# Layer 1's experts as seven block products over pairs of token tiles, with combined weights kept split in DRAM

## The chip, the cores and the metric

One Trainium2 chip, one of its cores. The core has five engines that run side by side and each take their own instructions in order: PE (TensorE, matmuls, with weight loads shown apart as PEld), DVE (VectorE), ACT (ScalarE), POOL (GpSimd) and SP (SyncE, which here issues all DMA transfers). The metric is the device time of one execution in microseconds (us), the median over runs.

## The reference

Input `x` is 4 sequences of 512 tokens with 1024 features, in fp32: 2048 tokens, 16 tiles of 128. Two layers follow one another, each with an attention part and an expert part, each behind a layer norm and added to `x`. What the change concerns is the last part:

```
x_q     = x[:, 179:-1, :]                      # x here is the normalised input of this part
routing = softmax(x_q.mean(axis=1) @ router_W.T + router_b)     # one row of 8 weights a sequence
base    = x @ W.T + b                                           # 1024 x 1024
t       = einsum("bsd,erd->bser", x, A)                         # 8 experts, rank 16: 128 columns
lora    = einsum("bser,eor,be->bso", t, B, routing) * 2
out     = base + lora                                           # added to the residual
```

Layer 0's expert part has the same base and low-rank products, but chooses two experts for each token (`route`). Layer 1's attention has 32 heads; its output projection is already computed in seven block products over two token tiles.

## The kernel before

Every product that matters is done in three matmuls (`matmul3`, L128 to L132): each fp32 operand is split into a high part in fp32r and a low rest, and low x high, high x low and high x high are accumulated. A split is a copy on ACT (the high part) and a subtraction on DVE or POOL (the rest).

The stages, in order: layer 0's attention; layer 0's experts, tile by tile (a loop over `order`); shared projections of layer 1's attention; its heads, with weight preparation and the output projection (`project`) interleaved as generators that `advance` steps; layer 1's experts. The scheduler under the kernel places instructions on each engine in nearly this order.

Layer 0's experts, around L430 to L460: per tile, `base` makes three column groups of `po` in PSUM (L130 to L132, 72 matmuls), the first group of tile s+1 before the routing of tile s. `turn0` normalises (`h`, L121) and transposes two tiles ahead (L143, then L125 on ACT and L126 on DVE). POOL adds the bias (L441). `finish` (L330) adds 9 low-rank matmuls to `po` and adds `po` to `x`. Six PSUM banks hold the groups of two tiles, so the first group of tile s+2 needs the bank that L330 of tile s reads. The results go to DRAM as `x_d` (L454). A buffer `raw` of 3072 columns serves as staging room at several places, one use after another; here it holds the weights `waT` from tile 8 on.

Layer 1's experts: its weight `w1` has 1024 + 128 columns and 8 chunks of 128 rows. `fetch_w1` (L668) loads two chunks at a time into `raw` and `prepare_w1` (L673 on ACT, L674 on DVE or POOL) splits them, among the last output projections (`project`, L798 to L847: loads `xs` at L815, split operands `cxh`, `cxl`, additions L843, stores L847). Tiles are loaded (`xt`, L1006), normalised and transposed three tiles ahead (`turn1`). The loop over `s` then runs `base` on three groups of 384 columns, the weighting of the low-rank input (`weigh`), and `finish`, which stores to the output. `mixture` makes the routing of a sequence from the sums of its tiles.

Some numbers of lines in the groups below: L251ff and L221 are layer 0's attention, L743 to L786 the heads of layer 1 (scores, transposes L767, context L783), L882 to L886 the preparation of output weights, L712 and L716 small tables through DRAM.

Of the kernel before, what the change touches and what calls it, by code (L numbers as in the profile page):

```python
# [38 lines left out]
W1_COLS = ((0, 384), (384, 768), (768, 1152))  # L39
# [3 lines left out]
def block_kernel(ctx: ExitStack, tc: tile.TileContext, a: dict, out: bass.AP):  # L43
# [308 lines left out]

    attn = ExitStack()
# [17 lines left out]
    with tc.tile_pool(name="b_h", bufs=2) as hp, tc.tile_pool(name="b_hTh", bufs=2) as hTh, \  # L371
# [54 lines left out]
        po = {0: base(hts[0], w0, W0_COLS, pop, slice(0, 3))}  # L426
        for s, t in enumerate(order):
            if s + 1 < NT:
                po[s + 1] = base(hts[s + 1], w0, W0_COLS, pop, slice(0, 1))
            q, k = divmod(s, NB)  # L430
            hw = weigh(po[s], routed(po[s]), ptp, wk) if s + 1 < NT else hw_last
            if s + 1 < NT:
                po[s + 1] += base(hts[s + 1], w0, W0_COLS, pop, slice(1, 2))
            if k == 1 and q + 1 < TPB:
                with tc.issue_after(normed[1].ins):
                    stats0[q + 1] = statistics([x[:, n * TPB + q + 1, :] for n in range(NB)])
            if s + 2 < NT:
                hts[s + 2] = turn0(s + 2)
            if s == NT - 1:
                hts1[1] = turn1(1, ptp)  # L440
            G.tensor_tensor(x[:, t, :], x[:, t, :], bias0, ALU.add)  # L441
            if s == NT - 2:
                hw_last = weigh(po[s + 1], routed(po[s + 1]), ptp, wk)
            if s + 1 < NT:
                po[s + 1] += base(hts[s + 1], w0, W0_COLS, pop, LAST)
            if s == NT - 2:
# [10 lines left out]
            if s == NT // 2:  # L457
# [203 lines left out]

    W1N = W1_COLS[-1][1]
    w1 = []

    def fetch_w1(ch, room, k):

        r = room[:, k * W1N : (k + 1) * W1N]
        nc.sync.dma_start(out=r, in_=a["w1"][ch])  # L668
        return r

    def prepare_w1(r, pool, eng):
        h, l = (pool.tile([P, W1N], FR, name=f"w1{len(w1)}{q}") for q in "hl")
        A.copy(h, r)  # L673
        eng.tensor_tensor(l, r, f32(h), ALU.subtract)  # L674
        w1.append((h, l))

    with ExitStack() as c2:
# [259 lines left out]
        for u in range(NU + 3):  # L937
# [38 lines left out]
            if u < NU:  # L976
# [8 lines left out]
                if (g, b, i) == (NG - 1, NB - 1, 0):  # L985
                    room = raw()
                    w1_raw = [fetch_w1(k, room, k) for k in range(2)]
# [8 lines left out]
        w1q = dp.enter_context(tc.tile_pool(name="d_wB", bufs=1))  # L996
        hTh = dp.enter_context(tc.tile_pool(name="d_hTh", bufs=4))
        hTl = dp.enter_context(tc.tile_pool(name="d_hTl", bufs=4))
        hp = dp.enter_context(tc.tile_pool(name="d_h", bufs=1))
        xtp = [dp.enter_context(tc.tile_pool(name="d_xA", bufs=4))]  # L1000
        ptp = dp.enter_context(tc.tile_pool(name="d_pt", bufs=2, space=PSUM))

        def fetch(s):
            xs[s] = xt = xtp[s % 6 // 4].tile([P, D], F32, name="xt")
            for k in range(2):
                nc.sync.dma_start(out=xt[:, k * 512 : (k + 1) * 512], in_=x_d[s][k])  # L1006

        xs, hts, sums, rw, po = {}, {}, {}, {}, {}

        def turn1(s):  # L1010
            b, j = divmod(s, TPB)
            h = hp.tile([P, D], F32, name="h")
            normalise(h, xs[s], *stats[s][0], stats[s][1])
            r0, r1 = max(Q_START - j * P, 0), min(Q_END - j * P, P)
            if r0 < r1:
                sums[j] = small.tile([P, ND, 1], F32, name=f"sum{j}")
            hts[s] = transposed(h, (hTh, hTl), ptp, (sums[j], r0, r1) if r0 < r1 else None)

        for s in range(TPB):
            fetch(s)  # L1020
# [4 lines left out]
        stats = {s: (mv, s) for s in range(TPB)}  # L1025
        prepare_w1(w1_raw[0], w1q, V)
        w1_raw += [fetch_w1(2, room, 0)]
        turn1(0)
        prepare_w1(w1_raw[1], w1q, G)
        w1_raw += [fetch_w1(3, room, 1)]  # L1030
        advance(filler, 7)
        turn1(1)
        prepare_w1(w1_raw[2], w1q, V)
        w1_raw += [fetch_w1(4, room, 0)]
# [160 lines left out]
```

## Time and profile before

| | us |
|---|---|
| median of 3 runs | 1829.35 |
| lowest and highest | 1826.6, 1829.43 |
| the profiled execution | 1828.0 |
| its span, first to last instruction | 1826.2 |
| PE busy in the span | 1751.3 (96%) |
| DVE, ACT, POOL busy | 1286.7, 832.1, 803.0 |
| mean granted TensorE clock | 0.991 of full speed |
| DMA moved | 191.33 MB, 105 GB/s in the mean |

The profile is of one execution. Busy times are those of each engine; a busy PE counts matmuls that overlap in its pipeline, so that the pace of matmuls is read from start to start. A row of a group reads: line, engine, operation, output and inputs with their shapes, count, then busy us and mean ns of one, then idle time of that engine just before, with what ended it. A row of the timeline begins with the start and the length in us. SPq stands for the queue of DMA issues. A line number in a group can be that of a helper, such as `matmul3`.

### The profile page before, as it was taken

To read this page: it belongs to the slowest core of one execution; us is meant where nothing else is said; L and a number is where in the kernel's file an instruction comes from. 1 tells how busy PE (TensorE), PEld (TensorE's weight loads), DVE (VectorE), ACT (ScalarE), POOL (GpSimd) and SP (SyncE) were. 2 spreads that over 40 slices of the span, in tenths; PEclk is the share of its full clock that TensorE was granted. 3 is DMA by queue.
4 is the path that set the end of the run, shared out by engine and by line. 5 is a ranking of instruction groups with operands and counts; after the bars stand their busy time and mean duration, and the time that the engine had idled before them with its cause. 6 is when DMAs were issued, how large, how long until landed. Compare 5 with 4: busy or idle time off the path is not lost.

```text
span 1826.2 us, 29837 instructions
## 1 busy us (share of the span) xinstructions
PE 1751.3 (96%) x10136; PEld 1479.7 (81%) x10136; DVE 1286.7 (70%) x3396; ACT 832.1 (46%) x2187; POOL 803.0 (44%) x724
## 2 busy tenths in 40 slices
PE   6979999999899999989999999999999999899999
PEld 6979999998568777757778757877757777799999
DVE  7775665676887777687777687777678777854441
ACT  6321111266665555555555465555465655411110
POOL 0351111101665665565666566566566565521110
PEclk9989999999999999999999999999999999999999
DMA  4220000235423324433324343333343233611111
GB/s 185 80 89 36 35 36 35 66 106 166 145 72 131 119 87 137 140 114 122 131 90 134 114 154 114 116 113 109 110 159 126 68 104 122 223 58 70 64 64 47
DMA packets 113464, 191.33 MB, mean 105 GB/s; under 512 B 20960, under 2 KB 51168, under 8 KB 111264
## 3 DMA queue, kind: packets, MB, share of 16 engines
q1 hardware_dynamic: 113312, 189.43, 31.2%
q8 instruction: 80, 1.31, 0.3%
q14 instruction: 72, 0.59, 0.1%
HBM read 131.70 MB, written 57.67 MB: 104 GB/s over the span
## 4 chain that ended last, share of the span: by engine, by line
PE 82%; DVE 6%; POOL 4%; ACT 3%; DMA 2%; issue 1%; SPq 0%; POOLq 0%; ACTq 0%; DVEq 0%
PE po L130 8%; PE po L131 8%; PE po L132 8%; PE psv L783 7%; PE pst L767 6%; PE pss L130 3%; PE pss L132 3%; PE pss L131 3%; PE pob L130 3%; PE poa L130 3%; PE psq L130 3%; PE psq L132 3%; PE psq L131 3%; PE pob L131 2%; PE poa L131 2%; PE poa L132 2%
## 5 line engine op out<-in xcount | busy, mean ns | idle before, releaser
L746 ACT ACTIVATE p<-p,mn 128x512 f32<-128x512 f32 (+3 forms) x512 | 284.1, 557 | 239.5 <-DVE mn L743 238.9
L553 POOL TENSOR_TENSOR qf<-qf,ropeT 64x512 f32<-64x512 f32 x128 | 167.7, 1310 | 206.0 <-ACT qf L549 204.7
L743 DVE CUSTOM_DVE_ANT_0 p<-pss,causal 128x512 f32<-128x512 f32 (+3 forms) x512 | 231.8, 487 | 23.8 <-PE pss L132 19.9
L767 PE MATMUL pst<-ident,p 128*128 128x128 f32 x1280 | 186.2, 275 | 4.6 <-DVE pT L769 4.3
L554 POOL TENSOR_TENSOR qf<-qf,t 64x512 f32<-64x512 f32 x128 | 165.8, 1295 | 46.0 <-DVE t L552 38.6
L767 PEld LDWEIGHTS pst<-ident,p 128*128 128x128 f32 x1280 | 154.2, 142 | 32.8 <-DVE pT L769 7.4
L769 ACT COPY pT<-pst 128x512 f32<-128x512 f32 x256 | 143.6, 578 | 65.1 <-PE pst L767 64.9
L783 PE MATMUL psv<-pT,k 128*64 128x384 f32 (+3 forms) x1024 | 165.5, 444 | 0.0
L130 PE MATMUL pss<-kT,ql 128*128 128x512 f32 (+2 forms) x384 | 144.0, 375 | 22.3 <-POOL ql L562 14.3
L562 POOL TENSOR_TENSOR ql<-qf,qh 128x384 fp32r<-128x384 f32 x128 | 132.8, 1038 | 57.9 <-DVE qh L561 53.4
L805 POOL TENSOR_TENSOR cxl<-s,cxh 128x256 fp32r<-128x256 f32 x128 | 96.1, 752 | 125.2 <-ACT cxh L804 121.4
L783 PEld LDWEIGHTS psv<-pT,k 128*64 128x64 f32 x1024 | 73.7, 138 | 87.3 <-issue 76.5
L130 PE MATMUL po<-w_h,hTl 128*128 128x384 f32 (+1 forms) x384 | 133.6, 348 | 0.0
L132 PE MATMUL pss<-kT,qh 128*128 128x512 f32 (+2 forms) x384 | 131.3, 342 | 0.0
L131 PE MATMUL pss<-kT,qh 128*128 128x512 f32 (+2 forms) x384 | 131.0, 341 | 0.0
L131 PE MATMUL po<-w_l,hTh 128*128 128x384 f32 (+1 forms) x384 | 130.6, 340 | 0.0
L132 PE MATMUL po<-w_h,hTh 128*128 128x384 f32 (+1 forms) x384 | 130.5, 340 | 0.0
L125 ACT CAST hwh<-pt 128x128 fp32r<-128x128 f32 x32 | 8.5, 266 | 230.3 <-PE pt L315 230.3
L769 DVE COPY pT<-pst 128x256 f32<-128x256 f32 x128 | 53.9, 421 | 80.1 <-PE pst L767 78.4
L130 PEld LDWEIGHTS pss<-kT,ql 128*128 128x128 f32 x384 | 72.7, 189 | 45.0 <-POOL ql L562 18.1
L441 POOL TENSOR_TENSOR x<-x,bias 128x1024 f32<-128x1024 f32 x16 | 38.2, 2397 | 154.4 <-DVE h L121 128.3
L549 ACT COPY qf<-psq 128x512 f32<-128x512 f32 x126 | 73.7, 585 | 64.9 <-PE psq L132 64.4
(550 smaller groups left out, 4820.3 us busy)
## 6 DMA issues: line engine op xcount, KB each, us to landing
xs<-x_d SPq DMA_DIRECT2D x128, 256.0 KB
x_d<-xs SPq DMA_DIRECT2D x128, 256.0 KB
qT<-q_d SPq DMA_DIRECT2D x16, 1024.0 KB
wo<-in_woT_dram SPq DMA_DIRECT2D x32, 512.0 KB
rb<-r_d SPq DMA_DIRECT2D x128, 128.0 KB
x<-in_x_dram SPq DMA_DIRECT2D x16, 512.0 KB
x_d<-x SPq DMA_DIRECT2D x32, 256.0 KB
kT<-kT_d SPq DMA_DIRECT2D x16, 512.0 KB
```

The lines of the kernel that those rows point to most:

```text
L130: T.matmul(ps, lhsT=al, rhs=bh, start=start, stop=False, **kw)
L131: T.matmul(ps, lhsT=ah, rhs=bl, start=False, stop=False, **kw)
L132: T.matmul(ps, lhsT=ah, rhs=bh, start=False, stop=stop, **kw)
L553: G.tensor_tensor(f[mid], f[mid], ropeT[mid, 0, :], ALU.mult)
L554: G.tensor_tensor(f[mid], f[mid], t2[mid], ALU.add)
L562: G.tensor_tensor(l, f[:, P:S], f32(h), ALU.subtract)
L743: V.tensor_tensor_reduce(out=to, in0=ps[:, 0:n], in1=causal[:, S - n : S], scale=1.0, scalar=-NEG, op0=ALU.add, op1=ALU.min, accum_out=mn[ ...
L746: A.activation(to, to, AF.Exp, bias=mn[:, i : i + 1], scale=-1.0, accum_out=rs[:, i : i + 1])
L767: T.transpose(ps[:, w : w + P], p[:, OF[i] + j * P : OF[i] + (j + 1) * P], ident)
L769: copy(pT[:, AT[js[0]] : AT[js[0]] + w], ps[:, 0:w])
L783: T.matmul(ps[n * KVR : (n + 1) * KVR, S - w : S], lhsT=k[:, j, :], rhs=pTs[u + n][:, AT[j] : AT[j] + w], start=(j == 0), stop=(j == TPB - 1))
L805: G.tensor_tensor(l, src, f32(h), ALU.subtract)
```

## The change

The weight of layer 1's experts, with its 128 low-rank columns in place 288 to 415, is 1152 columns wide. It is halved by columns (two problems `s` of 576), and each problem is a 2 x 2 block product: two token tiles by two halves of the 1024 features, times two halves of the features by two column blocks of 288 (`W1B`). Instead of eight block products there are seven, whose operands are sums of blocks: the weights b11, t1 = b12 - b11, t2 = b22 - t1, b22, t3 = b22 - b12, b21, t4 = b21 - t2, and on the token side a11, s1 = a21 + a22, s2 = s1 - a11, s4 = a12 - s2, s3 = a11 - a21, a12, a22.

The combined weights are made and split during layer 0's experts, one chunk and column half `u` for each of eight tiles, in `raw`, and written to 14 tensors in DRAM (`w1_d`). Two staging slots take the seven kinds in turn. Layer 1's experts load them whole: the first problem's seven into the left side of SBUF as attention closes, the second's into the right side after the last projection. `waT` is then loaded from tile 10 on instead of 8. The splits of `w1` at the former place are gone.

In layer 1's experts a pair of tiles goes through `STEPS`. Two PSUM banks a problem accumulate; after each product DVE adds the bank into the output tile `xo` (and its low-rank part into `inputs`). Pair 0 runs the first problem alone and then the second, so its operands are split twice; pairs 1 to 7 run both problems in each step. The low-rank product is done apart (`lora`), for both pairs of a sequence in the odd pair.

```diff
+W1B = (ER + D) // 4
+KINDS = ("b11", "t1", "t2", "b22", "t3", "b21", "t4")
...
+    def prepare_w1(room, u):
+        c, s = divmod(u, 2)
+        b11, b12, b21, b22, m1, m2 = (room[:, k * W1B : (k + 1) * W1B] for k in range(6))
+        def keep(kind, src, less=None):
+            if less is not None:
+                V.tensor_tensor(src, less[0], less[1], ALU.subtract)
+            n = 6 + 2 * (KINDS.index(kind) % 2)
+            h, l = (room[:, (n + k) * W1B : (n + k + 1) * W1B].bitcast(FR) for k in range(2))
+            A.copy(h, src)
+            (G if less is None else V).tensor_tensor(l, src, f32(h), ALU.subtract)
+            nc.sync.dma_start(
+                out=w1_d[kind, s][:, :, c, :],
+                in_=room[:, n * W1B : (n + 2) * W1B].rearrange("p (k n) -> p k n", k=2))
+        keep("b11", b11)
+        keep("t1", m1, (b12, b11))
+        yield
+        keep("t2", m2, (b22, m1))
+        keep("b22", b22)
+        yield
+        keep("t3", m1, (b22, b12))
+        keep("b21", b21)
+        yield
+        keep("t4", m2, (b21, m2))
+        if u + 1 < ND:
+            fetch_w1(room, u + 1)
+        yield
...
+        room1 = raw()
+        fetch_w1(room1, 0)
         for s, t in enumerate(order):
+            prep = prepare_w1(room1, s - 2) if 0 <= s - 2 < ND else iter(())
...
+            next(prep, None)
...
-            if s == NT // 2:
+            if s == ND + 2:
                 rawA = raw()
...
-                if (g, b, i) == (NG - 1, NB - 1, 0):
-                    room = raw()
-                    w1_raw = [fetch_w1(k, room, k) for k in range(2)]
...
+        def turn1(q, half):
+            for t in range(2):
...
+                    T.transpose(pt[:, c, :], hs[q][t][:, ch * P : (ch + 1) * P], ident)
+                blocks[t, half] = abp.tile([P, ND // 2, P], F32, name=f"a{t}{half}")
+                A.copy(blocks[t, half], pt)
...
+            for q in (0, *range(NP)):
+                a11, a12, a21, a22 = (blocks[k] for k in ((0, 0), (0, 1), (1, 0), (1, 1)))
+                yield split(a11)
+                s1 = add("s1", a21, a22, ALU.add)
+                yield split(s1)
...
-        prepare_w1(w1_raw[0], w1q, V)
-        w1_raw += [fetch_w1(2, room, 0)]
-        turn1(0)
...
+        norm(0, 0)
+        norm(0, 1)
+        advance(filler, 3)
+        for k in range(1, 7):
+            load_w1(KINDS[k], 0)
+            advance(filler, 2)
+            if k in (2, 3):
+                turn1(0, k - 2)
+            if k == 4:
+                fetch_h(1)
+                fetch_x(0)
+            advance(filler, 2)
+        ops = operands()
+        parts = [next(ops), next(ops)]
         advance(filler, 28)
...
+    bias1 = broadcast_rows(w1r, a["b1"], D, "bias1")
+    for kind in KINDS:
+        load_w1(kind, 1)
...
-    for s in range(NT + 1):
-        b, j = divmod(s, TPB)
...
-            po[s] = base(hts[s], w1, W1_COLS, pop, slice(0, 1))
...
+    def lora(q, t):
+        for k in range(2):
+            at = slice(k * 512, (k + 1) * 512)
+            ps = lop.tile([P, 512], F32, name="lo")
+            matmul3(ps, *hw[q, t], bt1[0][:, at], bt1[1][:, at], start=True, stop=True)
+            V.tensor_tensor(xo[q][t][:, at], xo[q][t][:, at], ps, ALU.add)
...
+    STEPS = (("b11", 0, True, (0, 0)), ("t1", 1, True, (1, 1)), ("t2", 0, False, (0, 1)),
+             ("b22", 1, False, (0, 1)), ("t3", 0, False, (1, 1)), ("b21", 1, True, (0, 0)),
+             ("t4", 0, False, (1, 0)))
+    def product(q, step, problems):
+        kind, bank, start, (t, half) = STEPS[step]
+        bank = (bank + q) % 2
+        h, l = parts.pop(0)
+        if (more := next(ops, None)) is not None:
+            parts.append(more)
+        for s in problems:
...
+            for c in range(ND // 2):
+                matmul3(ps, h[:, c, :], l[:, c, :], w[:, 0, c, :], w[:, 1, c, :],
+                        start=start and c == 0, stop=c == ND // 2 - 1, skip_group_check=True)
...
+            V.tensor_tensor(to, to, ps[:, skip:W1B], ALU.add)
...
+    for q in range(NP):
...
+        if q == 0:
+            for step in range(7):
+                product(0, step, (0,))
...
+        for step in range(7):
...
+            product(q, step, (0, 1) if q else (1,))
```

Four `next(prep, None)` stand in the loop of layer 0's experts: after the second column group, after the transposes of the tile two ahead, after the last column group, and after the stores of the tile.

## The prediction

> **What bounds the kernel now.** I read the busy time of each engine by stage first, then the pace of single matmuls, then what the idle VectorE (DVE) waits for, then the DMA queue. Columns of the first fence: stretch in us, its length, busy us and count of PE, PEld, DVE, ACT, POOL, then granted clock, DMA share, GB/s.
>
> ```profile
> 115.00:355.00 240.00, 239.52 (x1430) 237.41 (x1428) 143.81 (x474) 37.91 (x84) 39.82 (x20) 1.00 0.09 33
> 225.30:240.35 15.05, 15.05 (x92) 14.98 (x91) 8.09 (x27) 1.55 (x4) 2.39 (x1) 1.00 0.09 35
> 1541.00:1580.00 39.00, 32.55 (x158) 24.07 (x157) 35.75 (x49) 16.56 (x31) 19.82 (x18) 1.00 0.75 249
> 1580.00:1595.00 15.00, 12.19 (x68) 11.55 (x67) 8.39 (x19) 4.17 (x6) 8.52 (x4) 1.00 0.58 210
> 1595.00:1821.00 226.00, 224.43 (x1341) 222.92 (x1340) 97.02 (x237) 31.37 (x66) 33.20 (x14) 1.00 0.16 57
> ```
>
> Layer 0's experts (115 to 355) and layer 1's (1595 to 1821) are bound by TensorE: no idle time, one tile per 15.05 us. Between them, at the joint (1541 to 1595), PE idles 6.5 + 2.8 = 9.3 us. Three matmuls show what a narrower one is worth:
>
> ```profile
> 1639.83 0.28 PE L132 MATMUL po<-b1h,hwh 128*128 128x256 f32 x1
> 1639.95 0.34 PE L130 MATMUL po<-b1h,hwl 128*128 128x384 f32 x1
> 1640.13 0.33 PE L131 MATMUL po<-b1l,hwh 128*128 128x384 f32 x1
> ```
>
> From start to start a 256-wide one takes 0.120 us and a 384-wide one 0.174 (mean over the rows that follow), so columns cost 0.42 ns each plus about 13 ns; at 512 the attention's rows give 0.228, on the same line. A 288-wide one is then 0.1335.
>
> **Gain in the last stage.** Before: 16 tiles x 72 matmuls of 384 at 0.174 = 200.8 us. After: 8 pairs x 7 products x 2 column halves x 4 chunks x 3 = 1344 matmuls of 288 at 0.1335 = 179.4. The low-rank part was 9 matmuls a tile (6 x 0.174 + 3 x 0.120 = 1.40) and becomes 6 of 512 at 0.228 = 1.37. Transposes stay at 8 a tile. Sum: -21.4 - 0.6 = **-22.0 us**. That a weight load could hold the narrower matmuls back is excluded for 256 columns by the first row, and transposes, each with its own load, run at 0.109. At the end the last addition covers 288 columns after one product instead of following nine small matmuls: -0.5.
>
> **What the removed splits and the added ones cost.** L673/674 split eight chunks at the joint, five of them among the last projections. Their work goes to layer 0's stage: per tile, for eight tiles, 2 reads of 288 KB, 7 copies on ACT, 8 operations of 288 columns on DVE, 3 on POOL, 7 writes of 288 KB. Busy time alone fits: at 256 and 384 columns L330 takes 0.420 and 0.554, so 0.454 at 288, 3.6 us on DVE's 8.1 to 11.1; ACT +3.0 on 1.6; POOL +2.5 on 2.4; SP 72 issues of 0.33 to 0.45 us in 120; traffic 21 MB, 175 GB/s on 35. But only two staging slots exist, and four kinds (b11, t2, t3, t4) follow each other through one. Each round there is copy, subtraction, write, and the next copy waits for the write. The nearest rows:
>
> ```profile
> 624.15 0.32 SPq L847 DMA_DIRECT2D x_d<-xs  x1
> 627.12 0.32 SPq L815 DMA_DIRECT2D xs<-x_d  x1
> L804 ACT CAST cxh<-s 128x256 fp32r<-128x256 f32 x114 | 45.8, 402 | 21.3 <-PE pob L132 15.0 <-PE poa L132 6.1
> L805 POOL TENSOR_TENSOR cxl<-s,cxh 128x256 fp32r<-128x256 f32 x114 | 84.7, 744 | 110.2 <-ACT cxh L804 106.4 <-DVE t L552 2.9
> L330 DVE TENSOR_TENSOR x<-x,po 128x256 f32<-128x256 f32 x14 | 5.9, 420 | 32.1 <-PE po L132 32.1
> ```
>
> A 256 KB write issued at 624.15 lets the reload of its buffer go at 627.12: 2.97 us. ACT at 288 is 0.43 (402 ns at 256, 588 at 512), POOL 0.82 (1039 at 384). A DVE round is 0.43 + 0.45 + 2.97 + 0.1 for hand-overs (an estimate) = 3.95, b11's on POOL 4.3: the loop is 16.2 us a tile against PE's 15.05. This matters because DVE and ACT take their work in order. In the changed order the subtractions of t3 and t4 stand on DVE ahead of the next tile's routing and `h`, and t2's just ahead of the additions of L330, which free the PSUM bank of the next tile's first product. The last row is DVE's slack there: 32.1 us of waiting over 14, 2.3 each. What exceeds it, PE waits. Loss: 8 x 1.15 - 2.3 = **+7**. Bounds: a 1 KB write of L712 issued at 600.73 frees its reader at 602.08 (1.35), and with 0.7 for the data the loop is under 13, loss 0. The upper end takes these:
>
> ```profile
> L798 DVE TENSOR_TENSOR s<-cx 128x256 f32<-128x256 f32 x58 | 48.1, 829 | 14.4 <-POOL cxl L805 14.0
> L798 DVE TENSOR_TENSOR s<-cx,s 128x256 f32<-128x256 f32 x29 | 14.6, 505 | 0.8
> 1594.95 2.08 DVE L95 SCALAR_TENSOR_TENSOR nt<-mvd,nt 128x1 f32<-128x1 f32 x1
> 1591.15 5.86 POOL L1095 TENSOR_TENSOR xt<-xt,bias 128x1024 f32<-128x1024 f32 x2
> ```
>
> The same 256-wide operation takes 0.829 or 0.505, and one on a single column 2.08 while POOL's bias addition runs. Three DVE rounds 0.4 longer and one caught behind a bias addition (2.4) make 19.8 a tile: +36. I take the row of the same size of write, 7, since POOL is busy only a third of a tile.
>
> The Trainium skill (SBUF — State Buffer, section "SBUF: two separate sides") says why: DVE operations with two SBUF inputs and POOL's operations exclude each other for a whole instruction. The rows above agree (2.08 us for one column). By the rule every one of the eight added DVE operations may lose up to a POOL instruction, which speaks against the change; taken at its worst it gives the upper end, taken at POOL's share the 7.
>
> Its page DMA: Bandwidth & Descriptors, section "Anatomy of one DMA", gives 2.0 us plus bytes over 436 GB/s, 2.68 us for these writes (an estimate, for another issuing engine); by it the loop is 15.0 and the loss nothing, and the total would be 1811 instead of 1818. The measured 2.97 decides here.
>
> **The joint.** Removed: on the chain of waits a 3.65 us split on POOL (w11l) at 1546 and DVE's splits. Added: 14 loads of 1.18 MB. The first seven stand on SP among the last projections' loads and stores, from about 1549. The other seven can only be issued when the projection's memory is free, about 1580, behind the seventh of the first set and the bias.
>
> ```profile
> 5.00:10.00 5.00, 0.00 (x0) 0.00 (x0) 4.49 (x14) 2.12 (x5) 0.00 (x0) 1.00 1.03 420
> 1565.00:1570.00 5.00, 2.99 (x16) 2.47 (x17) 5.00 (x8) 2.19 (x6) 2.71 (x4) 1.00 0.99 348
> ```
>
> A full DMA moves 348 to 420 GB/s, so one lands every 2.9 to 3.4 us; the seventh at about 1606. Changed PE order: three products of pair 0 before the last five projection products, four after, then the second column half, with 21 matmuls of pair 1 before its last product. From 1579 to 1606 PE has 153 x 0.1335 + 16 transposes x 0.109 = 22.2 us of work in 27: idle 5. Before 1579 I keep 5 of the 6.5 idle us (the splits go, loads of `xs` queue behind weights). Together 10 against 9.3: **+1**. Range: -5 (all idle covered by early products) to +8 (rate 348 and the `xs` loads late by two weight loads).
>
> **Inside the last stage.** Per pair PE has 22.4 + 2.7 + 1.7 + 0.2 = 27.1 us. DVE gets 14 bank additions (ten of 0.454, four of 0.29 + 0.32: 7.0), four operand sums of 512 (L882, the same shape, means 1.10: 4.4), low-rank additions 2.7, norms 1.6, statistics 2.8, sums 1.8, weights 1.2, small ones 2.2: 23.7, 87%. POOL 7 x 1.3 + 2 x 2.4 = 13.9, ACT about 8. A bank must be added out before its next product, about 4.8 us later, and bursts of DVE work (statistics and norm, 4.4 us) come near that: **+3**, from 0 to 16 (DVE at 29 a pair, if operand sums take L886's worst 1.62 and the small ones wait for POOL).
>
> **Sum.** The profiled execution took 1828.0 us (span 1826.2): 1828.0 - 22.0 - 0.5 + 7 + 1 + 3 = 1816.5. The median 1829.35 is 1.35 above it: 1818.
>
> **Rivals.**
> A. Slower: the staging loop in layer 0 decides. It outweighs the other terms (-18.5) when a tile there exceeds 15.05 + (18.5 + 2.3)/8 = 17.65 us. With contended rounds (+1.2) and half a bias addition (+1.2) a tile takes 18.6, loss 26: 1837. For: 829 against 505, 2.08 us on one column. Against: POOL is idle two thirds of a tile. 0.20.
> B. DVE becomes the bound of the last stage, +12 instead of 3: 1827, about no change. For: 87%; against: 24 of these us have no order among them that PE needs at once. 0.12.
> C. Weights read back late, at 210 GB/s as in 1580 to 1595: 39 us for seven loads, PE +14: 1832. Against: the 420 row. 0.06.
> D. Nothing is lost, the loop hides and the joint fills: 1828.0 - 22.5 - 2 + 1.35 = 1805. 0.15.
> Forecast: 0.47.
>
> **Numbers.** 0.2% is 3.7 us and about what can be told from no change. Faster: forecast 0.44, D 0.15, a part of B 0.05: 0.64. Same: 0.03 + 0.06 + 0.03 of A and C: 0.12. Slower: 0.24. The range goes from D to A, 1804 to 1836; the forecast's own is 1811 to 1825.
>
> **What would show it.** Right: 288-wide matmuls 0.133 apart; tiles of layer 0 at about 16 us where weights are made, with idle PE before the first product put down to L330's line, and DVE waiting for a DMA or ACT; 5 us idle about 1580 to 1606; pairs of 27 to 28 us. Wrong: layer 0's tiles at 15.05 (D) or beyond 17.65 (A); pairs beyond 28.5 (B); loads under 300 GB/s (C); 288-wide matmuls above 0.14, which takes the gain itself.

## The result and the profile after

The changed kernel takes 1844.76 us (median of 4 runs, 1841.07 to 1847.17) against 1827.97 us for the kernel before on the same chip: ratio 1.009, 95% interval 1.007 to 1.011. It is 0.9% slower, with the whole interval above 1, where the forecast was 1818 and the range ended at 1836. Its profiled execution spans 1843.2 us, 17.0 more than before.

The same view as at the start of the prediction, for the changed kernel: stretch in us, its length, busy us and count of PE, PEld, DVE, ACT, POOL, granted clock, DMA share, GB/s. The stretches from 1580 on are moved to where the changed kernel has its joint.

```profile
115.00:355.00 240.00, 228.59 (x1342) 224.99 (x1341) 168.25 (x514) 55.34 (x127) 58.08 (x40) 0.99 0.36 123
1541.00:1580.00 39.00, 37.42 (x200) 28.46 (x200) 24.52 (x51) 16.67 (x44) 15.65 (x21) 1.00 0.66 227
1580.00:1595.00 15.00, 9.18 (x38) 8.03 (x37) 8.36 (x10) 3.05 (x6) 8.03 (x7) 0.71 0.84 338
1595.00:1640.00 45.00, 33.11 (x191) 31.05 (x190) 19.31 (x38) 9.61 (x16) 19.89 (x15) 0.83 0.83 319
1640.00:1838.00 198.00, 190.15 (x1365) 183.36 (x1364) 146.61 (x335) 55.07 (x107) 98.17 (x61) 1.00 0.30 99
```

Three things differ from before. Layer 0's experts (first row) now leave TensorE idle for 11.4 us, where it had none to speak of. Between 1580 and 1640 TensorE is idle for 17.7 us of 60, and it works there at a granted clock of 0.71 and 0.83. The last stage (last row) has 7.9 us of idle time.

Three marks in each trace cut the execution into parts: the start of the first `po` matmul of layer 0's experts, of the first and of the last `psq` matmul of the attention heads (query products), and the end of the span. "Staging part" below is from the first `po` to the first `psq` (layer 0's experts and the shared projection), "tail" from the last `psq` to the end (last heads, joint, last stage).

| us | before | after | difference |
|---|---|---|---|
| up to the first `po` | 110.5 | 112.6 | +2.1 (the same code; 110.0 to 113.3 over all runs) |
| staging part | 335.6 | 348.8 | +13.2 |
| heads | 1076.4 | 1075.2 | -1.2 |
| tail | 303.7 | 306.6 | +2.9 |

The tail can be taken apart further, by adding up TensorE's idle time and, in windows of 2.5 us, its busy time times (1 - granted clock):

| tail, us | before | after |
|---|---|---|
| TensorE's work at full clock | 289.3 | 266.8 |
| idle, at the joint | 9.3 | 19.3 |
| idle, in the last stage | 5.2 | 11.6 |
| lost to the half clock | 0.0 | 8.9 |

So the gain that the change was credited with is all there, 22.5 us of matmul work, and some 25 us of idle time and slow clock have come in its place. The joint here ends at 1595 before and at 1640 after. The idle time of the last stage goes to the end of the span, whose last 5.2 us hold 3.8 us of it (3.6 before); the last row of the windows above stops at 1838.

What TensorE waits for in the changed kernel, from the view of waits (engine, what it worked on and line, releaser: us in total, times, longest); the first row is from layer 0's experts, the others from the tail:

```profile
PE po L133 <- DVE x L333: 11.4, 8, 3.5
...
PE acc L133 <- DVE raw L1217: 8.0, 1, 8.0
PE acc L133 <- POOL al L1088: 5.6, 2, 3.8
PE pob L133 <- DVE xs L878: 5.2, 2, 4.0
```

L333 is the finish addition (L330 before), and L1217 the addition of a product's bank to its output tile. L1088 is GpSimd's low part of an operand, and L878 the projection's addition to `xs`. In the staging part as a whole TensorE's idle time rises by 10.9 us, from 2.2 to 13.1.

### The profile page after: what moved, and what is told of

Its sections match the earlier page's. It is cut to its first block, busy times and chain, and to the rows that moved or that the text cites. A ratio compares the mean times of both kernels' runs of the same rounds, so it can differ in the third digit from the quotient of the medians.

```text
span 1843.2 us, 30884 instructions
## 1 busy us (share of the span) xinstructions
PE 1739.8 (94%) x10280; PEld 1461.9 (79%) x10280; DVE 1364.5 (74%) x3563; ACT 878.9 (48%) x2290; POOL 899.4 (49%) x808
## 4 chain that ended last, share of the span: by engine, by line
PE 71%; DVE 11%; DMA 6%; POOL 4%; ACT 4%; issue 2%; SPq 0%; ACTq 0%; POOLq 0%; DVEq 0%
PE psv L818 7%; PE pst L802 6%; PE pss L133 3%; PE pss L135 3%; PE pss L134 3%; PE pob L133 3%; PE poa L133 3%; PE psq L133 3%; PE pob L134 3%; PE pob L135 3%; PE psq L135 3%; PE poa L134 3%; PE acc L133 3%; PE poa L135 3%; DMA w_t<-raw 3%; PE psq L134 2%
## 5 line engine op out<-in xcount | busy, mean ns | idle before, releaser
L604 POOL TENSOR_TENSOR qf<-qf,t 64x512 f32<-64x512 f32 x128 | 166.3, 1299 | 45.9 <-DVE t L602 38.6
L133 PE MATMUL po<-w_h,hTl 128*128 128x384 f32 (+1 forms) x384 | 134.4, 350 | 11.4 <-DVE x L333 11.4
L133 PE MATMUL psq<-qT,wql 128*128 128x512 f32 x252 | 101.7, 403 | 1.9 <-DVE t L602 1.9
L601 DVE TENSOR_TENSOR t<-psq,ropeT 32x512 f32<-32x512 f32 x126 | 87.7, 696 | 19.5 <-ACT qf L599 15.3
```

The source lines that it names most:

```text
L133: T.matmul(ps, lhsT=al, rhs=bh, start=start, stop=False, **kw)
L604: G.tensor_tensor(f[mid], f[mid], t2[mid], ALU.add)
```

## Experiments: which half of the change costs what

**Before plus the preparation alone (e1).** The loop of layer 0's experts is that of the changed kernel; the rest is the kernel before.

```diff
+        room1 = raw()
+        fetch_blocks(room1, 0)
         for s, t in enumerate(order):
+            prep = prepare_blocks(room1, s - 2) if 0 <= s - 2 < ND else iter(())
...
-            if s == NT // 2:
+            if s == ND + 2:
```

> The kernel before with one part of the change alone: layer 1's expert weights are combined, split and written to DRAM beside layer 0's experts, and nothing reads them; the last stage is that of before. Theory 1 (the marks of time in the two traces: first head's scores 15.3 us later, of which 2 at the first product): the staging alone costs 14 to 16 us, so 1842 to 1844. Rival (the prediction's own term): it costs 7, so 1835. Second rival: the 15 us are a shift that comes with something else in the changed kernel, and this run stands within 2 us of before, 1828.

Measured: 1841.75 us, ratio 1.0079 (1.0064 to 1.0095), 14.4 us over before. Its staging part is 348.5 us, its tail 303.2.

**The change without the preparation (e2).**

```diff
-            prep = prepare_w1(room1, s - 2) if 0 <= s - 2 < ND else iter(())
+            prep = iter(())
...
-            nc.sync.dma_start(out=f32(w), in_=w1_d[kind, s])
+            nc.sync.dma_start(out=f32(w), in_=w1_d["b11", 0])
```

> The changed kernel without the preparation beside layer 0's experts: one block is split and written once (four writes), and all fourteen loads of the last stage read that one DRAM tile, so the products are the right number and size on wrong weights. Theory 1 (staging costs about 15, the joint and the last stage together gain nothing): 1828 to 1831, level with before. Rival (staging 7 as predicted, so that the joint and the last stage cost more than they save): 1837 to 1838. Second rival (the joint suffers only because layer 0's stage ends late or leaves DMA queues behind): below 1822.

Measured: 1830.06 us, ratio 1.0014 (1.0004 to 1.0025). The staging part is 335.4 us, its length before, and the tail 305.8. The two halves add up: 14.4 for the preparation and 2.6 for the rest are the change's 17. Theory 1 holds, and the joint's trouble does not come from layer 0's stage ending late: without the preparation its tail still has 18.1 us of idle time at the joint and 9.6 of slow clock.

## Experiments: what the staging costs, and why

The prediction put the staging's cost down to the two staging slots, each of which waits for its write. Two runs test that.

**No writes (e3)**, the 56 writes to DRAM left out:

```diff
-            nc.sync.dma_start(
-                out=w1_d[kind, s][:, :, c, :],
-                in_=room[:, n * W1B : (n + 2) * W1B].rearrange("p (k n) -> p k n", k=2))
```

> The changed kernel with the preparation computed in full and its 56 writes to DRAM left out; the loads of the last stage read one DRAM tile as in the run without preparation. If the two staging slots and the writes that they wait for set the pace (waits of ScalarE's copies for the two writes, 66 us in sum in layer 0's experts): the stage falls back to about 3 us over before, total 1831 to 1834. If the added work itself sets it (VectorE's instructions ahead of the finish additions, slower beside GpSimd's subtractions): little changes, 1841 to 1845.

**A third slot (e4):**

```diff
-            n = 6 + 2 * (KINDS.index(kind) % 2)
-            h, l = (room[:, (n + k) * W1B : (n + k + 1) * W1B].bitcast(FR) for k in range(2))
+            n = KINDS.index(kind) % 3
+            slot = extra if n == 2 else room[:, (6 + 2 * n) * W1B : (8 + 2 * n) * W1B]
+            h, l = (slot[:, k * W1B : (k + 1) * W1B].bitcast(FR) for k in range(2))
```

> The changed kernel with a third staging slot for the split pieces (in a tile of its own), so that a piece waits for the write of three pieces ago in place of two. If the rounds of a slot (4 us each, 16 us a tile) set the stage: rounds per tile fall from 3.5 a slot to 2.33, the stage gains 8 to 12 us, 1833 to 1837. If the engines' own work sets it: gain under 3, 1842 to 1845.

Measured: without writes 1851.6 us (ratio 1.0128, 1.0109 to 1.0148), with three slots 1842.32 (1.0086, 1.0071 to 1.0102). The staging parts are 355.2 and 351.8 us, longer than the changed kernel's 348.8. (The seven traces that run this stage unedited, those of the changed kernel, e1, e6 to e8, e12 and e15, lie between 348.2 and 350.5, so that e4 shows no gain rather than a loss.) Without writes the units run closer together: between 135 and 155 us VectorE is busy for 18.6 us of 20 (13.5 in the changed kernel) and TensorE for 9.5 (16.5). So the slots are not what costs. If anything they spread the work out.

The timeline of the changed kernel shows what happens instead. Columns: start us, duration us, engine, line, operation, out<-in, and in brackets the idle time before it and its releaser. POOL's row is its bias addition to the tile.

```profile
143.25 1.62 DVE L377 TENSOR_TENSOR raw<-raw 128x288 fp32r<-128x288 f32 x1
144.91 0.46 DVE L373 TENSOR_TENSOR raw<-raw 128x288 f32<-128x288 f32 x1
145.28 1.34 DVE L333 TENSOR_TENSOR x<-x,po 128x256 f32<-128x256 f32 x3
...
142.21 2.34 POOL L489 TENSOR_TENSOR x<-x,bias 128x1024 f32<-128x1024 f32 x1 [1.15 <-DVE h L124]
...
145.75 0.62 PE L133 MATMUL po<-w_h,hTl 128*128 128x392 f32 x1 [3.50 <-DVE x L333]
```

A low-half subtraction of a prepared piece (L377, 0.46 us elsewhere) lasts until 144.87 us, 0.3 us beyond the end of POOL's bias addition, then a difference (L373) follows, and only then the finish additions, for which TensorE has waited 3.5 us. Two causes are mixed here: GpSimd holds a VectorE instruction, and prepared pieces stand ahead of the finish additions in VectorE's queue. Six runs bear on them.

**All subtractions on GpSimd (e5), and all on VectorE (e10).** One line each way:

```diff
-            (G if less is None else V).tensor_tensor(l, src, f32(h), ALU.subtract)
+            G.tensor_tensor(l, src, f32(h), ALU.subtract)      # e5
+            V.tensor_tensor(l, src, f32(h), ALU.subtract)      # e10
```

> The changed kernel with all seven low-half subtractions of a unit on GpSimd, where four were on VectorE. Theory (VectorE's in-order queue is the cost: in layer 0's experts it spends 21.7 us on these subtractions and waits 21.8 us for ScalarE's copies ahead of them, and the finish additions that free TensorE's banks stand behind): the staging falls from 14 us to 4 to 8, total 1834 to 1838. Rival (the port that VectorE and GpSimd share: the same subtractions cost as much from the other engine, 864 against 682 ns, and slow VectorE meanwhile): no gain, 1842 or more.

> The changed kernel with all seven low-half subtractions of a unit on VectorE, the opposite of the run that moved them all to GpSimd and lost 7 us. Theory A (GpSimd's work is what hurts, since a VectorE instruction beside it is held: 1.62 us in place of 0.46): 3 to 6 us gained, 1839 to 1842. Theory B (VectorE's in-order queue is what hurts; GpSimd lost because VectorE then waited for it, 27.9 us, before it could reuse a block): three more subtractions and waits per unit, 4 to 8 us lost, 1848 to 1853.

Measured: on GpSimd 1852.12 us (ratio 1.0123, 1.0092 to 1.0154), on VectorE 1839.3 (1.0068, 1.0045 to 1.0091). The staging parts are 357.5 and 345.4. My theory for e5 fell. Between its successors the two runs speak for A: from e5 to e10, with more VectorE work and less GpSimd work, the part is 12 us shorter. Against the changed kernel e10's own gain is not clear: the intervals of the two times overlap, and TensorE's idle time in the part, 11.0 us, lies within the 10.8 to 13.1 of the seven unedited traces. In e5 VectorE also waits 27.9 us for GpSimd before it may reuse a block, so not all of that loss is the hold.

**The preparation spread over twelve tiles (e9)**, two pauses for each unit:

```diff
             fetch_w1(room, u + 1)
         yield
+        yield
+        yield
...
-            if s == ND + 2:
+            if s == 3 * ND // 2 + 2:
```

> The changed kernel with the same preparation spread over twelve tiles of layer 0's experts in place of eight (a unit of seven pieces lasts one and a half tiles; the shared projection's weights, which use the same staging memory, are fetched four tiles later). Theory (what costs is how dense VectorE's in-order queue gets: its busy share goes from 12.6 to 14 to 19 us in 20, and only where it is dense do the finish additions come late): the staging falls from 14 us to 7 or less, 1837 or less. Rival (each piece costs the same wherever it stands): 1843 to 1846.

Measured: 1844.62 us (ratio 1.0089, 1.0061 to 1.0117), staging part 348.5. No gain: bunched, as in e3, the work costs more, but spread out it costs no less, and the rival holds.

**The unit behind its tile's finish additions (e11)**, an order for VectorE alone; the four calls of `next(prep, None)` in the tile go:

```diff
-            next(prep, None)
...
-            finish(x[:, t, :], po.pop(s), hw, W0_COLS, (b0h, b0l))
+            added = finish(x[:, t, :], po.pop(s), hw, W0_COLS, (b0h, b0l))
+            with tc.issue_after(added.ins):
+                for _ in prep:
+                    pass
```

> The changed kernel with each unit's VectorE instructions queued behind the finish additions of its tile (a fixed order on VectorE, no other engine's order is set), so that none of them stands ahead of the additions that free TensorE's banks. Theory (order in the queue is the cost: TensorE's 11.4 us of waits in layer 0's experts are all for those additions): the staging falls to 3 to 6 us, 1832 to 1836. Rival (the next in line, the routing's small instructions and the transposes' low halves, come late in their place): 1842 to 1848.

Measured: 1840.65 us (ratio 1.0069, 1.0042 to 1.0096), staging part 345.8, a gain of 3 us in the part where 7 or more were expected, and a time between the theory's and the rival's. Its timeline shows why it is not more:

```profile
207.93 2.67 DVE L378 TENSOR_TENSOR raw<-raw 128x288 fp32r<-128x288 f32 x1
...
216.30 1.89 DVE L453 SCALAR_TENSOR_TENSOR rw<-one,w,rw 128x8 f32<-128x8 f32 x1
...
207.90 2.39 POOL L488 TENSOR_TENSOR x<-x,bias 128x1024 f32<-128x1024 f32 x1 [3.22 <-DVE h L124]
...
215.82 2.35 POOL L488 TENSOR_TENSOR x<-x,bias 128x1024 f32<-128x1024 f32 x1
```

A 288-column subtraction takes 2.67 us and a routing instruction on 8 columns 1.89 (0.23 when alone). Each starts within 0.5 us of the start of a bias addition on POOL and ends within 0.4 us of its end. Later work in the queue, the finish additions among it, moves back.

**Both edits (e13), and the bias addition in quarters (e14).** e13 is e10 and e11 together; e14 is the changed kernel with:

```diff
-            G.tensor_tensor(x[:, t, :], x[:, t, :], bias0, ALU.add)
+            for c0 in range(0, D, 256):
+                at = slice(c0, c0 + 256)
+                G.tensor_tensor(x[:, t, at], x[:, t, at], bias0[:, at], ALU.add)
```

> The changed kernel with both edits that helped: all seven low-half subtractions on VectorE, and a unit's VectorE instructions behind the finish additions of its tile. Theory (two causes, GpSimd's hold and the order in the queue): the gains of 5.5 and 4 us add up, 1834 to 1836. Rival (one cause seen twice, VectorE blocked ahead of the finish additions): the larger gain alone, 1838 to 1841.

> The changed kernel with layer 0's bias addition on GpSimd (1024 columns, 2.42 us, one a tile) cut into four of 256 columns, nothing else. Theory (a VectorE instruction that starts beside it ends only when it ends: 2.67 us for 288 columns in place of 0.46, 1.89 us for 8 columns in place of 0.22): holds fall to a quarter, 3 to 6 us gained, 1839 to 1842. Rival (the pieces follow one another at once and hold as long): no gain, 1844 to 1847.

Measured: e13 1837.37 us (ratio 1.0052, 1.0039 to 1.0065), staging part 344.1, between its two forecasts; e14 1841.3 (1.0069, 1.0044 to 1.0094), staging part 345.6, as its theory had it. Cutting POOL's instruction gains 3 us in the part although POOL's bias additions take longer (64 of 805 ns, 49.4 us, in place of 16 of 2418 ns, 38.6). e13's part gains 4.7 where its two edits alone gained 3.4 and 3.0. With quarters on top (e16, below) the part is 340.4 us, and what the preparation costs has fallen from 13.2 us to 4.8. VectorE's subtraction shows the hold going; group rows of e13 and of e16, which differ in this stage by the quarters alone (operation, shapes, count | busy us, mean ns | idle before it):

```profile
L378 DVE TENSOR_TENSOR raw<-raw 128x288 fp32r<-128x288 f32 x56 | 34.4, 620 | 14.3 <-ACT raw L377 13.9
```

```profile
L378 DVE TENSOR_TENSOR raw<-raw 128x288 fp32r<-128x288 f32 x56 | 26.7, 482 | 14.2 <-ACT raw L377 13.8
```

The mean falls from 620 to 482 ns. TensorE's waits for L333 are 11.4 us in the changed kernel, 7.1 in e13 and in e14, and 1.0 in e16, where two waits for VectorE's routing instructions (2.0 and 1.6 us) have come in; its idle time in the part is 8.8 us in e14 and 6.7 in e16. Each version has one trace, and the time of a single edit (e10, e11, e14) has an interval that overlaps the changed kernel's. Clear of it are e13 and e16.

## Experiments: the joint

In the changed kernel the longest single wait has a plain chain. Timeline rows of VectorE, SP (SPq is its DMA issue) and POOL:

```profile
1609.23 0.29 DVE L1213 COPY inputs<-acc 128x128 f32<-128x128 f32 x1 [5.91 <-DMA x_d<-xs]
...
1601.68 0.64 SPq L882 DMA_DIRECT2D x_d<-xs  x1
...
1610.50 2.37 POOL L1186 TENSOR_TENSOR raw<-raw,bias 128x1024 f32<-128x1024 f32 x1 [9.25 <-DMA bias<-in_b_dram]
```

The buffer `inputs` lies where an `xs` buffer lay, whose last store was issued at 1601.68 among the weights' loads and landed at 1609.2. VectorE's copy waits for it, the bank's addition waits behind the copy, and TensorE's fourth product waits for the bank. That the two buffers share memory is concluded from the releaser that the profile names.

**`inputs` in a pool of its own (e6):**

```diff
+        inpd = dp.enter_context(tc.tile_pool(name="d_in", bufs=2))
...
-        inputs[q] = wk.tile([P, 2, ER], F32, name="inputs")
+        inputs[q] = inpd.tile([P, 2, ER], F32, name="inputs")
```

> The changed kernel with the small buffer for the low-rank inputs in a pool of its own, in memory that the projection's buffers do not use, so that the first copy into it has no transfer to wait for (8.0 us of idle TensorE at 1601.8 to 1609.8, put down to a store of xs that landed at 1609.2). Theory (this wait alone holds the joint): 8 us and some half-clock stretch are gained, 1833 to 1836. Rival (the bias addition on GpSimd, whose data landed at 1610.5 and which takes 4.7 us, is next in line for the fourth product's addition): gain 0 to 4, 1841 to 1845.

Measured: 1844.59 us (ratio 1.0095, 1.0068 to 1.0122), tail 306.2. The rival: the same product now waits 10.45 us, and starts at 1610.95.

**And the first pair's bias later (e7):**

```diff
             for step in range(7):
                 product(0, step, (0,))
-                if step == 2:
-                    biased(0)
+                if step == 6:
+                    biased(0, (0,))
...
+            if step == 2 and q == 0:
+                biased(0, (1,))
```

> The run before with one more edit: the bias is added to the first pair's two tiles behind their seventh product and behind the second half's third product, in place of between the third and fourth. Theory (the two waits stand in line): both go, and the fourth to seventh products of the first half run at 1602 to 1609 with no idle TensorE: 1832 to 1836, against 1841 to 1845 if the run before shows its rival. Rival (the second half's weights, seven loads that share the DMA queue with the stores and land one per 3 us up to 1630, are the next wait): gain under 4 us over the changed kernel.

Measured: 1841.71 us (ratio 1.0074, 1.0049 to 1.01), tail 302.9. That is 3 us less than the changed kernel, with intervals that overlap. Both waits are gone, and the next in line is one that neither forecast had: transposes of the second pair at 1609.09, for which TensorE waits 4.17 us. The profile names no releaser there; by the times it is VectorE's sum over the previous transposes, which stands behind an operand sum that waited for GpSimd. Behind it come loads:

```profile
1615.72 0.37 PE L133 MATMUL acc<-wt,al 128*128 128x288 f32 x1 [0.81 <-DMA wt<-w_t]
1618.51 0.37 PE L133 MATMUL acc<-wt,al 128*128 128x288 f32 x1 [0.96 <-DMA wt<-w_t]
1621.30 0.37 PE L133 MATMUL acc<-wb,al 128*128 128x288 f32 x1 [0.96 <-DMA wb<-w_b]
```

The second half's products start 2.79 us apart, one for each load of 1.18 MB (423 GB/s), while a product is 1.6 us of work.

**The first pair's products behind the projection (e8):** e7, with

```diff
             for step in range(7):
-                product(0, step, (0,))
+                with tc.issue_after(ends[0].ins), tc.issue_after(ends[1].ins):
+                    product(0, step, (0,))
```

where `ends` are the projection's latest matmul and addition.

> The run before with the first pair's products, and VectorE's sums and copies for them, queued behind the last projection product's matmul and addition (in the changed kernel three of them stand ahead of its last five, and VectorE's sums wait there for GpSimd's splits while an addition that frees a projection bank waits behind them, 4.0 us of idle TensorE). Theory (the early products cost more than they fill): 2 to 5 us less than the run before. Rival (they fill time in which the projection waits anyway): 3 to 6 us more than the run before.

Measured: 1844.5 us (ratio 1.0087, 1.0064 to 1.0111), tail 306.4, 3 us more than e7. That is on the rival's side (the projection now waits 8.2 us at once, time that the early products filled), but the intervals of the two runs overlap. The theory's gain of 2 to 5 us is not there.

**Loads first (e12):** e7, with `tc.high_priority()` around all loads of these weights but the first.

> The run with inputs apart and the bias later, with one more edit: the fourteen loads of layer 1's weights get priority, so that SP issues the first half's before the last batch's stores and the second half's before the last of them. Theory (SP's in-order queue holds the loads: the first half's last two were issued at 1598 and 1601 behind stores that waited 9.4 us for VectorE, the second half's from 1603): 4 to 8 us less than that run's 1841.7, so 1834 to 1838. Rival (the transfers themselves are the limit, 14 loads at 2.8 us; ahead of the last batch's loads of x they make the projection wait instead): 1841 or more.

Measured: 1851.56 us (ratio 1.0132, 1.0107 to 1.0157), tail 316.3. The rival: six weight loads now stand ahead of the last loads of `xs`, and one projection product waits 15.2 us.

**Half the bytes (e15):** e7, with

```diff
-            nc.sync.dma_start(out=f32(w), in_=w1_d[kind, s])
+            part = slice(0, 2 - s)
+            nc.sync.dma_start(out=f32(w[:, part]), in_=w1_d[kind, s][:, part])
...
-                matmul3(ps, h[:, c, :], l[:, c, :], w[:, 0, c, :], w[:, 1, c, :],
+                matmul3(ps, h[:, c, :], l[:, c, :], w[:, 0, c, :], w[:, 1 - s, c, :],
```

> The run with inputs apart and the bias later, with half the bytes for the second half's weights: its seven loads bring the high parts alone, and the products use these for the low parts too, so that the number and size of the products stay and the output columns 512 to 1023 are wrong. Theory (with the waits gone, the transfers bind the joint: the DMA engines are full from 1600 to 1630 and the second half's products follow loads that land 2.8 us apart): 5 to 9 us less than that run's 1841.7, 1833 to 1837. Rival (SP's issue order and GpSimd's splits bind it): within 2 us, 1840 to 1843.

Measured: 1839.53 us (ratio 1.0067, 1.0045 to 1.009), tail 300.8, about 2 us under e7 where 5 to 9 were expected. The waits for loads of the second half have fallen from 3.7 to 0.9 us, but the 4.17 us before the transposes and 4.4 for GpSimd's splits (4.6 in e7) stay, and one of 4.4 for the mixture's sums comes in.

**All edits that helped (e16), and two more (e17, e18).** e16 is e13, e14 and e7 together. e17 adds:

```diff
-            load_w1(KINDS[k], 0)
+            for kind in ((), KINDS[1:2], KINDS[2:3], KINDS[3:4], KINDS[4:7], (), ())[k]:
+                load_w1(kind, 0)
```

and e18 moves the splitting of the low-rank output weights from the first half's sixth product to behind the second half's fifth.

> The changed kernel with all edits that helped: subtractions on VectorE, behind the finish additions, the bias addition in quarters, inputs apart and the first pair's bias later. Theory (staging and joint are apart in time, so their gains add): 1844.8 less 9 (order and hold), less 0 to 4 (quarters), less 3 (joint), 1829 to 1833, still not faster than before. Rival (the gains overlap): 1835 to 1839.

> The combined run (1832.05) with one more edit: the last two loads of the first half's weights issued right behind the fifth and ahead of the load of the second pair's tiles, in place of behind stores of the projection that waited for VectorE. Theory (SP's order holds the loads; the DMA engines stand at 0.4 to 0.6 for 10 us ahead of the second half's loads): up to 5 us less, 1827 to 1830. Rival (the queues of VectorE and GpSimd between the halves set it): 1831 to 1833.

> The run before with one more edit: the low-rank output weights are split on VectorE (1024 columns, 2.30 us beside GpSimd's splits, which take 3.52 us for two there in place of 2.6) behind the second half's fifth product, where the first half's sixth had it. Theory (the queues between the halves set it; TensorE's 4.17 us wait for transposes ends when VectorE's sums come behind this split): 2 to 4 us less than the run before. Rival (what comes later in the queue takes the place): within 1 us of it.

| run | time, us | ratio (95%) | staging part | tail | idle at joint, slow clock in tail |
|---|---|---|---|---|---|
| e16 | 1832.05 | 1.0019 (1.0006 to 1.0031) | 340.4 | 305.1 | 18.2, 7.5 |
| e17 | 1833.46 | 1.0019 (1.0005 to 1.0033) | 339.8 | 305.8 | 18.7, 8.1 |
| e18 | 1833.12 | 1.0023 (1.0010 to 1.0036) | 339.1 | 304.9 | 18.6, 7.9 |

e16 is the best version of the change, and it is still 0.2% slower than before. Of the 10.8 us between its trace and the changed kernel's, 8.4 lie in the staging part; its tail is within 2 us of the changed kernel's, so that e7's 302.9 has to be read with that much scatter. Its time is where its theory had it, but the 3 us that the theory counted for the joint are not shown. e17 and e18 gain nothing over it by their ratios, as their rivals had it. (The tail of the changed code, unedited, came out at 304.3 to 306.6 in ten traces.) In e17 the two loads are issued 13 and 16 us earlier than in e16, counted from the last `psq`, and in their place TensorE waits for the second pair's normalised tiles and for GpSimd (waits of e17). The wait of 4.17 us that e18 was to end is already gone there:

```profile
PE acc L133 <- POOL al L1091: 7.9, 3, 5.0
PE pt L1069 <- DVE h L124: 5.1, 2, 3.0
```

**What stays open.** The joint's idle time (in the first 103.4 us of the tail, as for the changed kernel) was 18.1 to 20.9 us in every run with the new last stage whose tail I took apart but e12 (28.6), whichever wait was taken away. There is no single binding resource there that these runs found: VectorE's queue, GpSimd's splits, SP's order and the transfers take turns within a few us of each other. An order of work that relieves all of them at once was not tried.

## Why the prediction was wrong, step by step

**Gain in the last stage, -22.0 and -0.5: right.** The matmuls of 288 columns start 0.133 us apart at full clock, and TensorE's work in the tail fell from 289.3 to 266.8 us, by 22.5.

**Staging, +7: wrong, 13.2.** The step that failed is the choice of the mechanism: a loop over two slots, "16.2 us a tile", of which what exceeds VectorE's slack of 2.3 us is lost. Tiles with preparation did get longer, 15.05 + 13.2 / 8 = 16.7 us, and the idle time is at L333 as forecast, but e3 and e4 show that the slots do not set it. What sets it, by e5, e10, e11, e13, e14 and e16, is VectorE's queue: instructions held beside GpSimd's, and new work ahead of the finish additions. With both relieved (e16) 8.4 of the 13.2 us go; the other 4.8 were not tested further. The text had the right mechanism in its rows, 2.08 us for one column beside POOL's bias addition, and used it for the upper end only, "since POOL is busy only a third of a tile". A third of the time is enough: there is one bias addition a tile, eight VectorE instructions were added that can run into it, and whatever is caught delays all that stands behind it, the finish additions first. The Trainium skill (SBUF — State Buffer, section "SBUF: two separate sides") states this rule of an exclusive port that one of the two engines holds for a whole instruction; the rows of e11 and the gain of e14 agree with it.

**The joint, +1: wrong, by most of the error.** Idle time there rose by 10.0 us, and 8.9 us went to the half clock, for which the sum had no term. The step that failed is "153 x 0.1335 + 16 transposes x 0.109 = 22.2 us of work in 27: idle 5". It took the arrival of the weights as the only supply. The loads came a little faster than predicted (one per 2.8 us in e7, against 2.9 to 3.4), but the second half's were issued from 1603 on, behind the projection's last stores. And the products between had other suppliers: a bank that VectorE must empty, a buffer over memory that a store still read, GpSimd's splits, the bias. Which of them binds stays open; the runs show that taking one away brings up the next.

**Inside the last stage, +3: too small, 6.4.** Idle time in it is 11.6 us against 5.2. Two pairs take 57 us, 28.5 a pair, at the edge that was named for rival B. But VectorE is not the bound, at 74% where 87% was predicted; the waits are for single chains (the weighted low-rank inputs, 4.3 us in three waits).

**The sum.** -22.5 + 13.2 + 10.0 + 8.9 + 6.4 is +16.0; the time before the first `po` (+2.1) and the heads (-1.2) make it +16.9, against 17.0 measured. The prediction had -11.5.

**The rivals.** A had the right place and, in its contended rounds, the right cause; at 13.2 us it stays below the 18.5 that it needed to decide, and the result is slower because the joint lost more still, 10.0 us idle and 8.9 to the slow clock. C is excluded by the loads' 423 GB/s (e7), D by both parts. None of the rivals had two terms going wrong together, though the range's upper end (1836) was built from one of them alone. Slips in the text change nothing of this: 16 x 72 x 0.174 is 200.4 and not 200.8, a pair adds up to 27.0 and not 27.1, D and A come to 1805 and 1837 where the range says 1804 and 1836, and the write that is taken as one of the same size has 256 KB, where the new ones have 288.

## What to carry to other kernels

Work that is moved under a stage bound by TensorE costs by its place in the in-order queue it joins and by the longest instruction on the engine that can hold that queue, not by its busy time; look for the longest GpSimd instruction there, shorten it, and put the new work behind the instructions that free TensorE's banks. Here that took away two thirds of the cost and not all. A saving of TensorE's work between two stages is worth only what the suppliers around it can follow: list every one that would be next, with its time, before counting the saving. Where TensorE starts to have gaps, add a term for its clock, by how the gaps lie and not by their sum alone (next section).

## What the runs showed of the hardware that was not expected

Gaps at the joint cost twice. Matmul rows of the changed kernel, around a wait of 1.84 us:

```profile
1580.43 0.29 PE L135 MATMUL acc<-wb,ah 128*128 128x288 f32 x1
1582.56 0.40 PE L133 MATMUL acc<-wt,al 128*128 128x288 f32 x1 [1.84 <-POOL al L1088]
...
1583.21 0.44 PE L133 MATMUL acc<-wt,al 128*128 128x288 f32 x1
1583.45 0.44 PE L134 MATMUL acc<-wt,ah 128*128 128x288 f32 x1
...
1586.58 0.29 PE L133 MATMUL acc<-wt,al 128*128 128x288 f32 x1
1586.71 0.29 PE L134 MATMUL acc<-wt,ah 128*128 128x288 f32 x1
```

For some 3.3 us after the gap the same matmul starts every 0.24 us in place of 0.133. After the wait of 8.00 us it does so for 3.7 us, and after the wait of 3.97 us the projection's matmuls of 512 columns start every 0.43 us in place of 0.23 for 4.9 us. The Trainium skill (TensorE: Matmul & The Clock Gate, section "Part 1: The HAM clock gate") gives a half clock after an idle window of about 3.4 us and a return after a busy one as long. The length of the slow stretches fits that, but here the clock also fell after 1.84 us, so a gap need not be a whole window long; the measurement decides.

The traces show more of the pattern. In this tail the granted clock changes only on a grid of steps of 3.41 us: slow stretches begin at 1582.87 and 2, 7 and 14 steps later. How much of one step TensorE is idle decides the clock of the next. Two neighbouring steps of the changed kernel, then one of the kernel before (stretch in us, its length, TensorE's busy us and count, granted clock, DMA share, GB/s):

```profile
1579.46:1582.87 3.41, 1.56 (x12) 1.00 1.02 405
1582.87:1586.29 3.42, 3.42 (x16) 0.50 1.00 402
...
1565.42:1568.83 3.41, 1.82 (x12) 1.00 0.99 337
```

A step that is idle for 54% is followed by one at half clock. In the kernel before, 47% is the most in any step at its joint, and the clock stays full: its 9.3 us of idle time are spread over pieces that never fill half a step, and so it lost nothing. Over the tails of all 20 traces, each cut on its own grid, none of the 398 steps at full clock with less than 50% idle time was followed by a slow one, all 59 with more than 60% were, and 9 of the 18 between. A slow step was followed by a full one in all 10 cases with at most 16% idle time, and in none of 45 with 17% or more. Ahead of the heads the clock fell in four traces after a step with 36% idle time, so this is not the whole rule.
